# First output product's sums brought forward on VectorE, and the first norm's statistics spread over six pairs

## The chip, the cores and the metric

One core of one Trainium2 chip runs the whole kernel. The metric is the device time of one execution in microseconds. Before the change it is 1449.13 us, the median of 3 runs (1449.05 to 1449.21).

## The reference, cut to what matters

The input is x of shape (4, 1024, 512), that is 4096 tokens of width 512, and a context of 4 batches of 64 rows. Weights and results are float32.

```python
def reference(x, ctx, g_xattn, g_ffn, w_q, w_k, w_v, w_o, w_gate, w_up, w_down):
    # 16 heads of 64; keys and values come from the 64 context rows; causal mask on positions 0..63
    x = x + tanh(g_xattn) * cross_attention(layernorm(x), ctx, ctx, w_q, w_k, w_v, w_o)
    # gate, up and down projections of width 1536 with 16-bit activations and 4-bit weights
    x = x + tanh(g_ffn) * quantised_ffn(layernorm(x), w_gate, w_up, w_down)
    return x

def layernorm(x):
    return (x - mean(x)) / sqrt(var(x) + 1e-5)
```

Each of the two layer norms needs the variance of every token's row. The kernel turns the first norm's scale into a factor of the softmax's exponent (`rstd1`), so the scores are computed from raw x and the first norm is only needed when a maximum is scaled and an exponential is taken.

## The kernel before

**Stages.** A set-up stage builds the products of the context with the weights: for each batch the score matrices `m_all` and the value matrices `vwo`. The attention stage then runs over 16 *pairs* q = 0 to 15; a pair is two tiles of 128 tokens, four pairs make a batch. After it come the gate products, the up products and the down products. The change touches the end of the set-up and the attention stage.

**A pair.** Both matrix products of a pair are done in seven half-size products instead of eight, with sums around them (in the style of Strassen and Winograd). While pair q is attended, the scores of pair q+1 are made. TensorE's order is written by hand (`tc.manual_schedule`) and is, within pair q:

1. the score products 1, 6, 2, 5 of pair q+1 (L423);
2. the first turning: eight transposes of the softmax weights of pair q's first tile (L668);
3. the score products 7 and 3;
4. the second turning: the same for pair q's second tile;
5. the score product 4;
6. from q = 2 on, the transposes of two normalised tiles of an earlier group (L743);
7. the output products 1, 6, 2, 7, 5, 4, 3 of pair q (L702).

Each score product is copied (ScalarE, L429) or added (VectorE, L431) into the tile `e`. Softmax of each tile (L444 to L467) takes the masked sum where a batch begins (L444), a maximum (L449), its scaling by `rstd1` (L459), 16 exponentials, one for each head, with accumulated sums (ScalarE, L461), a reciprocal (L466), and a product with it over 128x1024 values (L467). Only then can that tile be turned. After both turnings four sums over 128x512 (L674 to L677) make the operands `eT` of the output products.

**The sums of the output products.** In `attend`, output product 1 is copied to `r` (L708). The result of each other product is added onto the token tiles `x1` and `x2` (L710), and `r` is added to the right half of `x1` after product 6 (L713) and to all of `x2` after product 2 (L716). The products 6, 7 and 4 use one PSUM bank, `oq`, one after the other: each waits until the add of the one before has read it. The add of product 7 goes onto `x2` and so comes after L716.

**Other work in the loop.** `batch_sums` (L401 to L406) makes the operand sums of a later batch, `turned_chunk` (L230 to L272) dequantises and transposes a chunk of the gate weights, `score_left` (L370 to L378) prepares the left operands of later scores, and `renormed` makes the second norm of tiles already attended (ScalarE, L730; VectorE, L738).

**Statistics and roots.** A *group* is four tiles, that is two pairs; there are eight. `stats_of(g)` loads the four tiles of group g again by SyncE's queue, one at a time into two buffers `xe` (L342), and runs a statistics and an aggregate instruction for each (L329, L332). `norm_of` turns variances into reciprocal roots: VectorE adds epsilon (L175), ScalarE takes a square root with a table load of its own (L178), and VectorE refines it (L180 to L189). In the kernel before, groups 0 and 1 have their statistics in the set-up, groups 2 and 3 ahead of the loop, groups 4 to 7 behind the pairs 0 to 3. Roots are taken for group 0 in the set-up ("a0"), for groups 1 to 3 ahead of the loop ("a1") and for groups 4 to 7 together with the second norm's root at q = 5 ("b2").

**What sets the order.** On engines other than TensorE a scheduler in the language places the instructions when the program is built, from their priorities; `tc.high_priority(SOON)` puts what it wraps ahead of other ready work, and `tc.issue_after` holds work back behind one instruction. On the chip each engine runs its list in that order.

Of the kernel before, what the change touches and what calls it, by code (L numbers as in the profile page):

```python
# [12 lines left out]
ALU = mybir.AluOpType  # L13
# [14 lines left out]
def kernel(  # L28
# [137 lines left out]
    def norm_of(pool, parts, tag):  # L166


        with tc.high_priority(SOON):
            n = sum(k.stop - k.start for _, _, _, k in parts)  # L170
            ve = pool.tile([P, n], F32, name=f"ve_{tag}", tag="ve")
            at = 0
            for rstd, off, mv, k in parts:
                w = slice(at, at + k.stop - k.start)
                nc.vector.tensor_scalar(ve[:, w], mv[:, k, 1], EPS, None, ALU.add)  # L175
                at = w.stop
            s = pool.tile([P, n], F32, name=f"s_{tag}", tag="vs")
            nc.scalar.activation(s, ve, AF.Sqrt)  # L178
            r = pool.tile([P, n], F32, name=f"r_{tag}", tag="vr")
            nc.vector.reciprocal(r, s)  # L180
            nc.vector.tensor_tensor(r, ve, r, ALU.mult)
            nc.vector.tensor_tensor(s, s, r, ALU.add)
            nc.vector.tensor_scalar(s, s, 0.5, None, ALU.mult)
            at = 0
            for rstd, off, mv, k in parts:
                w = slice(at, at + k.stop - k.start)
                nc.vector.reciprocal(rstd[:, k], s[:, w])
                if off is not None:
                    nc.vector.scalar_tensor_tensor(  # L189
                        off[:, k], mv[:, k, 0], -1.0, rstd[:, k], ALU.mult, ALU.mult  # L190
                    )
                at = w.stop
# [152 lines left out]
    def first_norm(*groups):  # L345
        return [(rstd1, None, mv1, of_group(g)) for g in groups]
# [124 lines left out]
    with tc.tile_pool(name="su", bufs=1) as su, tc.tile_pool(  # L471
# [129 lines left out]
                nc.sync.dma_start(out=xe, in_=tokens_of(g))  # L601
                group_stats(su, g, xe, True)

        norm_of(su, first_norm(0), "a0")
        for b in range(2, B):
            for k in range(2):
                nc.gpsimd.dma_start(out=m_d[b][k], in_=m_all[b][k])
# [4 lines left out]
        left[0] = score_left(0)  # L612
        for _ in batch_sums(0, 0):
            pass
        on_vector = []

        def value_matrix(b, hp, ps):

            for j in range(2):
                half = slice(j * D, (j + 1) * D)  # L620
                to = j if b % 2 == 0 else 1 - j
                nc.tensor.matmul(
                    ps[to * D : (to + 1) * D, :], vT[half, hp, b * KL : (b + 1) * KL],
                    wo[hp // 4][half, hp % 4, :], start=True, stop=True,
                )
            dst = vwo[b][hp // 4][:, hp % 4, :]
            if b != B - 1 or hp % 2 == 0:
                nc.scalar.activation(dst, ps, AF.Copy, scale=tanh_g[0])
            else:
                on_vector.append(nc.vector.tensor_scalar(dst, ps, tanh_g[0], None, ALU.mult))  # L630

        for hp in range(HP):
            for b in range(2, B):
# [6 lines left out]
    with tc.tile_pool(name="ps_s", bufs=1, space=PSUM) as ps_s, tc.tile_pool(  # L640
# [39 lines left out]
        def attend(q, a):  # L680

            b = right[1][q // QPB]
            g, i = divmod(2 * q, GRP)
            x1, x2 = xg[g][:, i, :], xg[g][:, i + 1, :]
            bank = {
                k: ps_o.tile([P, 2, HH], F32, name=f"{k}{q}", tag=k) for k in ("opn", "oq")
            }

            bank = {"op": bank["opn"][:, 0], "on": bank["opn"][:, 1], "oq": bank["oq"][:, 0]}
            r = pa.tile([P, HH], F32, name=f"r{q}", tag="r", bufs=1)  # L690

            def finished(t, x):
                nc.gpsimd.dma_start(out=x1_d[t], in_=x)
                stats(pa, x, mv2[:, t, :], f"b{t}")

            for k, at, start, dst in (
                (1, "op", True, None), (6, "oq", True, x1[:, RIGHT]), (2, "op", False, x1[:, LEFT]),
                (7, "oq", False, x2[:, RIGHT]), (5, "on", True, x2[:, RIGHT]),
                (4, "oq", False, x2[:, LEFT]), (3, "on", False, x1[:, RIGHT]),
            ):  # L700
                for h in range(HP // 2):
                    nc.tensor.matmul(  # L702
                        bank[at], a[k][:, h, :], b[k][:, h, :],
                        start=start and h == 0, stop=h == HP // 2 - 1, skip_group_check=True,
                    )
                with tc.high_priority(SOON):
                    if k == 1:
                        nc.scalar.copy(r, bank[at])  # L708
                    else:
                        ins = nc.vector.tensor_tensor(dst, bank[at], dst, add)  # L710

                if k == 6:
                    nc.vector.tensor_tensor(x1[:, RIGHT], x1[:, RIGHT], r, add)  # L713
                if k == 2:
                    v = x2.rearrange("p (n h) -> p n h", n=2)
                    nc.vector.tensor_tensor(v, v, r.unsqueeze(1).to_broadcast([P, 2, HH]), add)  # L716
                if k == 4:
                    finished(2 * q + 1, x2)
            finished(2 * q, x1)
            return ins.ins  # L720
# [38 lines left out]
        def next_left(q):  # L759
# [2 lines left out]

        ahead = scores(
            0, {6: values, 2: values, 5: lambda: values(lambda: next_left(1)), 7: values, 3: values},
            score_banks(0),
# [2 lines left out]
        next(firsts)  # L770
        next(firsts)
        softmax(0, ahead)
        with tc.issue_after(on_vector[-1].ins):
            for g in (2, 3):
                stats_of(g)
        norm_of(pa, first_norm(1, 2, 3), "a1")
        for q in range(NQ):
            b, k = divmod(q, QPB)
            turns = weights_turned(q, ahead)

            def turn():
                next(turns)
                return next(turns)


            if 0 < b < B - 1:
                if k == 0:
                    fetched(m_all[b + 1], m_d[b + 1], f"mb{b + 1}")
                if k == QPB - 1:
                    fetched(vwo[b + 1], vwo_d[b + 1], f"vb{b + 1}")  # L790
            if q == 0:
                load_group(1)
            if q % 2 == 0 and q // 2 + 2 < NG:
                load_four(xf, q // 2 + 2, xb, "x")
            if q + 1 < NQ:
                a = []
                behind = {5: turn, 3: lambda: (a.append(turn()), next_left(q + 2))}
                if q == 0:
                    behind = {**dict.fromkeys((1, 6, 2), values), 3: turn, 4: behind[3]}
                ahead = scores(q + 1, behind, score_banks(q + 1))  # L800
                if q == 0:
                    for _ in firsts:
                        pass
                softmax(q + 1, ahead)
            if q + 1 == NQ:
                turn()
                a = [turn()]
            if q > 1:
                for t in (2 * q, 2 * q + 1):
                    renormed(t - GRP)  # L810
            if q % 2 == 1 and q // 2 + 2 < NG:
                load_group(q // 2 + 2)
            if q + 1 == NQ:
                for p in range(UPB - 2):
                    ag.append(weight_sums(wgT, sg_t, p, "g"))
            added = attend(q, a[0])
            with tc.issue_after(added):
                if b + 1 < B and k in (1, QPB - 1):
                    for _ in batch_sums(b + 1, k // 2):
                        pass  # L820
            if q < NG - 4:
                stats_of(q + 4)

            if q == NQ - 2:
                norm_of(pa, [second_norm(slice(last, last + 2))], "c0")
            if q % 2 == 1 and q + 1 < NQ:
                g = q // 2
                parts = [second_norm(of_group(g))]
                if q == 5:
                    parts += first_norm(*range(4, NG))  # L830
                norm_of(pa, parts, f"b{g}")

            if 0 < q <= IC:
                oc = (q + 3) % IC
                turned_chunk(pa, oc, wgT, "g", q < 4)
                if oc > 3 and oc % 4 == 3:
                    nc.gpsimd.dma_start(out=wg_d[oc // 4 - 1], in_=wgT[oc // 4])
            if q % 4 == 0 and q < IC:
                load_four(w_gate, (q // 4 + 1) % (IC // 4), wgT, "g")
            if q == IC:  # L840
                load_four(w_up, 0, wuT, "u")
                for j in (1, 2):
                    wgT[j] = slot([P, HC, 4 * P], f"wgTb{j}")
                    nc.sync.dma_start(out=wgT[j], in_=wg_d[j - 1])
            k = q - IC
            if 0 < k < 3:
                for oc in range(2 * k - 2, 2 * k):
                    turned_chunk(pa, oc, wuT, "u")
# [705 lines left out]
```

## Time and profile before

| What | Value |
|---|---|
| median of 3 runs | 1449.13 us |
| the profiled execution's own time | 1452.2 us |
| its span | 1450.4 us |
| TensorE busy (PE) | 1406.2 us, 97% of the span |
| VectorE busy (DVE) | 1155.3 us, 80% |
| ScalarE busy (ACT) | 690.7 us, 48% |
| attention loop, from the first score product of pair 1 to that of pair 15 | 90.6 to 499.1 us |

The numbers come from one profiled execution. TensorE is the engine that is nearly always busy, so what counts is the time in which it stands idle and the time in which it is granted half its clock. In the timeline view a row gives the start, the length, the engine, the line, the instruction, what it writes and reads, the shape and the count; in brackets stands the idle time before it and what ended it. Rows on one engine overlap a little: the cost of an instruction in a row of others is the distance from its start to the next start.

### The profile page before, as it was taken

The numbers are of one execution on the slowest core, as the hardware profiler recorded it, in microseconds if no ns is written. First come the engines' busy times: TensorE is split into PE (matmuls) and PEld (weight loads), VectorE is DVE, ScalarE is ACT, GpSimd is POOL, SyncE is SP. The second block draws the span as 40 slices with busy tenths as digits, with TensorE's granted clock in tenths as the row PEclk, the third lists the DMA queues.
The fourth block names the chain that finished last, engine by engine and source line by source line (L and its number), as shares of the span: only waits on it lengthen the run. The fifth ranks groups of instructions, "written<-read, shape, count | busy, mean of one in ns | idle before, by whom it ended". The sixth has DMA issues, their size and how long they took to land. (4 is left out here: it accounts for less than half of the span.)

```text
span 1450.4 us, 15457 instructions
## 1 busy us (share of the span) xinstructions
PE 1406.2 (97%) x4884; PEld 857.6 (59%) x4884; DVE 1155.3 (80%) x2153; ACT 690.7 (48%) x1658; POOL 97.5 (7%) x191
## 2 busy tenths in 40 slices
PE   8998998999999989999999999999999999999999
PEld 6635665667667675444444444444444548888887
DVE  2777889898898899799985579888888897666632
ACT  3646576768768752000000049987886532222200
POOL 0100000000000001000000000000000110111110
PEclk9999999999999999999999999999999999999999
DMA  9675346436414215692323438958557475554321
GB/s 287 235 210 124 90 149 151 133 109 160 117 65 131 106 41 209 182 365 99 130 88 115 145 141 339 375 218 319 218 217 261 175 288 184 186 187 171 132 73 44
DMA packets 191385, 252.72 MB, mean 174 GB/s; under 512 B 125636, under 2 KB 125892, under 8 KB 185284
## 3 DMA queue, kind: packets, MB, share of 16 engines
q1 hardware_dynamic: 165828, 149.98, 33.1%
q0 software_dynamic: 18560, 76.56, 13.8%
q10 hardware_dynamic: 6912, 25.17, 4.3%
q8 instruction: 38, 0.62, 0.2%
q14 instruction: 47, 0.39, 0.1%
HBM read 142.61 MB, written 109.05 MB: 174 GB/s over the span
## 5 line engine op out<-in xcount | busy, mean ns | idle before, releaser
L461 ACT ACTIVATE e<-e,mx,rstd 128x64 f32<-128x64 f32 x416 | 177.0, 429 | 7.2 <-DVE mx L459 7.1
L886 PE MATMUL pqup<-t,wuT 128*128 128x512 f32 x192 | 91.2, 597 | 4.6 <-DVE raw_up L907 2.7
L423 PE MATMUL s<-t,xs 128*128 128x512 f32 x192 | 92.4, 604 | 0.3 <-DVE e L431 0.3
L902 ACT COPY raw_gate<-ppgate 128x512 f32<-128x512 f32 x24 | 14.1, 586 | 142.3 <-PE ppgate L886 142.3
L461 ACT ACTIVATION_READ_ACCUMULATOR e<-e,mx,rstd 128x1 f32 x416 | 78.8, 189 | 0.0
L1421 PE MATMUL ep<-wdT,upe 128*128 128x256 f32 x336 | 77.1, 379 | 0.0
L1347 ACT ACTIVATE uie<-upe,inv_up 128x1024 int16<-128x1024 f32 x48 | 53.8, 1145 | 47.7 <-DVE upe L1351 25.9
L702 PE MATMUL oq<-t,eT 128*128 128x256 f32 x256 | 64.6, 398 | 11.2 <-DVE xg L710 10.0
L1421 PE MATMUL eq<-tw,upe 128*128 128x256 f32 x312 | 72.5, 379 | 0.0
L431 DVE TENSOR_TENSOR e<-s,e 128x512 f32<-128x512 f32 x80 | 54.5, 682 | 19.3 <-PE s L423 18.9
L1421 PEld LDWEIGHTS ep<-wdT,upe 128*128 128x128 f32 x336 | 63.8, 190 | 9.1 <-DVE x1e L1400 0.2
L886 PE MATMUL ppup<-xu,wuT 128*128 128x512 f32 x144 | 67.7, 592 | 0.0
L1147 ACT ACTIVATE ar<-raw_up 128x1024 f32<-128x1024 f32 x46 | 48.3, 1052 | 40.1 <-DVE raw_up L1071 40.1
L1080 DVE TENSOR_REDUCE am_gu<-raw_up 128x1 f32<-128x512 f32 x92 | 62.4, 682 | 5.5 <-ACT raw_up L902 4.0
L886 PEld LDWEIGHTS pqup<-t,wuT 128*128 128x128 f32 x192 | 35.6, 189 | 52.3 <-issue 32.5
L894 ACT COPY raw_gate<-ppgate 128x512 f32<-128x512 f32 x24 | 14.1, 586 | 109.7 <-PE ppgate L886 75.9
L1351 DVE SCALAR_TENSOR_TENSOR upe<-uie,inv_o,gse 128x1024 f32<-128x1024 int16 (+1 forms) x50 | 60.5, 1236 | 5.1 <-ACT uie L1347 4.8
L1421 PEld LDWEIGHTS eq<-tw,upe 128*128 128x128 f32 x312 | 59.2, 190 | 8.3 <-DVE c L1439 0.3
L702 PEld LDWEIGHTS oq<-t,eT 128*128 128x128 f32 x256 | 50.3, 199 | 20.5 <-DVE xg L710 11.6
L423 PE MATMUL s<-m_all,xs 128*128 128x512 f32 x128 | 59.8, 597 | 1.5 <-DVE vwo L630 0.9
L886 PE MATMUL pqgate<-t,wgTb 128*128 128x512 f32 x128 | 60.2, 592 | 0.0
L423 PE MATMUL s<-mb,xs 128*128 128x512 f32 x128 | 59.0, 593 | 0.8 <-ACT e L429 0.8
(347 smaller groups left out, 3139.0 us busy)
## 6 DMA issues: line engine op xcount, KB each, us to landing
gate_d<-raw_gate ACTq DMA_DIRECT2D x48, 512.0 KB, 2.6
gt<-gate_d SPq DMA_DIRECT2D x48, 512.0 KB, 4.7
upe<-up_d SPq DMA_DIRECT2D x24, 1024.0 KB, 6.1
up_d<-raw_up POOLq DMA_DIRECT2D x46, 512.0 KB, 3.5
gse<-gsi_d SPq DMA_DIRECT2D x24, 512.0 KB, 4.0
gsi_d<-q SPq DMA_DIRECT2D x44, 256.0 KB, 2.7
wxT<-in_x_dram SPq DMA_DIRECT2D x128, 64.0 KB, 2.9
xg<-in_x_dram SPq DMA_DIRECT2D x8, 1024.0 KB, 6.6
```

The source lines that it names most:

```text
L423: nc.tensor.matmul(bank[at], a[k][:, h, :], b[k][:, h, :], start=start and h == 0, stop=h == HC // 2 - 1, skip_group_check=True,)
L431: nc.vector.tensor_tensor(dst, bank[at], other, add)
L461: nc.scalar.activation(ei[:, h, :], ei[:, h, :], AF.Exp, bias=mx[:, h : h + 1], scale=root, accum_out=sm[:, h : h + 1],)
L702: nc.tensor.matmul(bank[at], a[k][:, h, :], b[k][:, h, :], start=start and h == 0, stop=h == HP // 2 - 1, skip_group_check=True,)
L886: nc.tensor.matmul(bank[at], a[k][:, h, :], b[k][:, h, :], start=start and h == 0, stop=h == HC // 2 - 1, skip_group_check=True,)
L894: nc.scalar.copy(r0[:, 1, :], bank["pp"])
L902: nc.scalar.copy(r0[:, 0, :], bank["pp"])
L1080: nc.vector.tensor_reduce(am_gu[:, c, u : u + 1], r[:, c, :], AX.X, ALU.max, apply_absolute_value=True,)
L1147: nc.scalar.activation(ar, raw[u], AF.Abs)
L1347: nc.scalar.activation(ui, up[:, i, :], AF.Copy, scale=inv_u)
L1351: ins = nc.vector.scalar_tensor_tensor(o[:, i, w], ui[:, w], c_o, gs[:, i, w], ALU.mult, ALU.mult)
L1421: nc.tensor.matmul(bank[at], a[u // 2][k][:, u % 2, q % 2, :], w_of[u // 2][k][:, u % 2, :], start=start and u == 0, stop=u == UPB - 1, sk ...
```

## The change

It has two parts.

- The two adds of `r` in `attend` (L713, L716) get the high priority that the other sums have.
- The first norm's statistics and roots move. Group 1 gets its root together with group 0, in the set-up. The statistics of groups 2, 3, 4, 5, 6, 7 are placed behind pairs 0, 1, 2, 4, 6, 8. Their roots are taken in the same `norm_of` calls as the second norm's, at the first odd pair after the one behind which the statistics stand. The separate root "a1" and the hold behind the last value matrix's scaling are gone.

```diff
-        norm_of(su, first_norm(0), "a0")
+        norm_of(su, first_norm(0, 1), "a0")
...
-                on_vector.append(nc.vector.tensor_scalar(dst, ps, tanh_g[0], None, ALU.mult))
+                nc.vector.tensor_scalar(dst, ps, tanh_g[0], None, ALU.mult)
...
-                if k == 6:
-                    nc.vector.tensor_tensor(x1[:, RIGHT], x1[:, RIGHT], r, add)
-                if k == 2:
-                    v = x2.rearrange("p (n h) -> p n h", n=2)
-                    nc.vector.tensor_tensor(v, v, r.unsqueeze(1).to_broadcast([P, 2, HH]), add)
+                with tc.high_priority(SOON):
+                    if k == 6:
+                        nc.vector.tensor_tensor(x1[:, RIGHT], x1[:, RIGHT], r, add)
+                    if k == 2:
+                        v = x2.rearrange("p (n h) -> p n h", n=2)
+                        nc.vector.tensor_tensor(
+                            v, v, r.unsqueeze(1).to_broadcast([P, 2, HH]), add
+                        )
...
+        stats_behind = {2: 0, 3: 1, 4: 2, 5: 4, 6: 6, 7: 8}
...
-        with tc.issue_after(on_vector[-1].ins):
-            for g in (2, 3):
-                stats_of(g)
-        norm_of(pa, first_norm(1, 2, 3), "a1")
...
-            if q < NG - 4:
-                stats_of(q + 4)
+            for k, at in stats_behind.items():
+                if at == q:
+                    stats_of(k)
...
                 parts = [second_norm(of_group(g))]
-                if q == 5:
-                    parts += first_norm(*range(4, NG))
+                parts += first_norm(*(k for k, at in stats_behind.items() if at in (q - 1, q - 2)))
                 norm_of(pa, parts, f"b{g}")
```

More of the change, by code (lines that the diff above doesn't have):

```diff
@@ L614 @@
             pass
-        on_vector = []
         def value_matrix(b, hp, ps):
```

## The prediction

> **What bounds the kernel now.** I read the waits of TensorE first, then its timeline, then the windows of the pairs, then VectorE's timeline where TensorE waits. TensorE is busy for 97% of the span, so a gain must come out of its idle time or its clock. The waits, longest in total first:
>
> ```profile
> PE oq L702 <- DVE xg L710: 10.0, 4, 4.0
> PE ps_e L668 <- DVE e L467: 6.1, 4, 2.8
> ...
> PE ps_e L668 <- DVE mx L459: 3.3, 1, 3.3
> ```
>
> Two places in a pair: the output products that share the bank `oq`, held by VectorE's adds, and the turnings, held by the softmax. Where they lie (rows with a gap only, but for the second):
>
> ```profile
> 138.86 1.94 PE L668 MATMUL ps_e<-ident,e 128*128 128x128 f32 x8 [3.26 <-DVE mx L459]
> 140.59 3.62 PE L423 MATMUL s<-t,xs 128*128 128x512 f32 x4
> ...
> 183.59 3.78 PE L702 MATMUL oq<-t,eT 128*128 128x256 f32 x8 [3.59 <-DVE xg L710]
> ...
> 244.72 3.78 PE L702 MATMUL oq<-t,eT 128*128 128x256 f32 x8 [4.00 <-DVE xg L710]
> ...
> 302.82 1.99 PE L702 MATMUL oq<-t,eT 128*128 128x256 f32 x8 [1.19 <-DVE xg L710]
> 318.64 1.07 PE L668 MATMUL ps_e<-ident,e 128*128 128x128 f32 x8 [0.93 <-DVE e L467]
> ```
>
> After each of the three long gaps a product takes about 3.7 us instead of 1.9: half the clock. The windows of pairs 1, 2, 4 and 5, each from its first score product to the next pair's (columns: length, busy PE, PEld, DVE, ACT, POOL, then the granted clock):
>
> ```profile
> 124.26:156.56 32.30, 29.04 (x101) 19.29 (x100) 22.51 (x45) 26.93 (x118) 1.09 (x2) 0.89 0.47 114
> 156.56:189.96 33.40, 29.81 (x109) 20.34 (x108) 31.81 (x68) 19.42 (x63) 1.08 (x2) 0.90 0.43 109
> ...
> 217.02:251.24 34.22, 30.22 (x109) 20.35 (x108) 32.79 (x73) 23.52 (x85) 1.62 (x3) 0.90 0.62 140
> 251.24:277.97 26.73, 26.73 (x109) 18.44 (x108) 20.32 (x38) 21.37 (x84) 1.62 (x3) 1.00 0.43 111
> ```
>
> An undisturbed pair takes 26.73 us (25.86 before pair 2, without the 0.87 us of L743). What a pair takes above that is its excess: pair 0 2.94 (its four gaps), pair 1 6.44, pair 2 6.67, pair 3 0.32, pair 4 7.50, pair 6 1.67, pair 7 1.12, pair 10 2.72, pair 11 1.54, pair 13 0.27, in all 31.2 us. A long gap costs itself and about 3.1 us of clock (6.67 - 3.59; 6.44 - 3.26 gives 3.2). A gap of 2.80 us at 530.92 left the clock at 0.91 over 520 to 540, some 1.8 us; gaps up to 1.35 us cost nothing more.
>
> In pairs 2 and 4 VectorE is busy for 31.8 and 32.8 us, more than an undisturbed pair lasts. There the order on VectorE makes the gap. In pair 2:
>
> ```profile
> 177.34 0.41 DVE L710 TENSOR_TENSOR xg<-opn,xg 128x256 f32<-128x256 f32 x1
> ...
> 179.14 1.21 DVE L449 TENSOR_REDUCE mx<-e 128x16 f32<-128x1024 f32 x1
> 180.27 0.67 DVE L738 TENSOR_REDUCE am_x<-xm 128x1 f32<-128x512 f32 x1
> ...
> 181.59 0.41 DVE L713 TENSOR_TENSOR xg<-xg,r 128x256 f32<-128x256 f32 x1
> 181.93 0.68 DVE L716 TENSOR_TENSOR xg<-xg,r 128x512 f32<-128x512 f32 x1
> 182.53 0.70 DVE L370 STREAM_TRANSPOSE xs<-wxT 128x512 f32<-128x512 f32 x1
> 183.16 0.38 DVE L710 TENSOR_TENSOR xg<-oq,xg 128x256 f32<-128x256 f32 x1
> ```
>
> Product 7's add (183.16) comes 5.8 us after product 2's; TensorE needs it within 1.73.
>
> **Costs.** From start to next start on VectorE: L431, L329, L738, L67x 0.60; L710, L713 0.33; L449, L467, L40x 1.13; L444 1.20; L370 0.62; L466 0.16; L459 0.14; L332 0.09. One head's exponential 0.42, a copy on ScalarE 0.47 to 0.53, L730 0.76, a table load 1.28. Adding up the old order from a pair's last output add to the maximum's scaling gives 21.7, 22.8 and 20.0 us in pairs 2, 4 and 6; the trace has 21.5, 22.7 and 19.95. So the new order, which the built program shows, can be added up likewise.
>
> **The root "a1" goes.** It sat on ScalarE before pair 1's exponentials (load 108.91, reload 119.06); the first exponential came at 120.35. Without it and with eight statistics fewer ahead, the maximum of pair 1 is scaled near 109.3 instead of 118.8, and its weights are ready some 3 us before the turnings want them. Pair 1's 6.44 go. In pair 0 the sum that output product 6 needs comes about 0.45 earlier: excess 2.5.
>
> **The adds of r.** In pairs 2, 4 and 6 the new order leaves 2.2, 1.6 and 1.6 us of VectorE's work between the adds of products 2 and 7, so the waits on `oq` go: 6.67, 7.50 and most of 1.67 us. Pair 2 gets a small gap for it: the second operand sum (L675) ends at 17.4 us in the pair, product 6 could start at 16.4: 1.05.
>
> **What is late next.** The same order puts VectorE's normalisation of the second tile (L467) far back in the pairs 3, 5, 7 and 11, whose softmax begins in pairs 2, 4, 6 and 10. There the scaling of the maximum, which starts the exponentials, comes at 24.3 (before 21.7), 21.2 (23.4), 21.2 (20.2) and about 25 us (21.2), while the pair is shorter. From 24.3: load 1.28, 32 exponentials 13.4, two score copies 0.9, two weight copies 1.05, one L730 0.76 end at 41.7, 14.0 us into pair 3. The second turning wants its tile at 11.19 (six products of 1.72 and one turning of 0.87). And in all four pairs the last thing ahead of the normalisation is the add of score product 3, which itself cannot start before 11.39. Behind it, up to the end of L467 (1.22):
>
> - pair 3: L431 0.60, L738 0.59, L444 1.20, L329 0.60, L466 0.16, L332 0.09, L329 0.60, L467 1.22 = 5.06; with 0.2 from TensorE and 0.05 back, a gap of 5.3.
> - pair 5: L431, L466, L449, L467 = 3.11; gap 3.35.
> - pair 7: L431, L466, L329, L467 = 2.58, and two L370 ahead push it by 0.5: gap 3.35.
> - pair 11: L431, L375, L444, L466, L376, L467 = 3.85, VectorE 0.4 behind: gap 4.5.
>
> In the old order only one or two short steps stood there; in pair 7, the worst with 11:
>
> ```profile
> 316.24 0.68 DVE L431 TENSOR_TENSOR e<-s,e 128x512 f32<-128x512 f32 x1
> 316.84 0.24 DVE L466 RECIPROCAL rs<-sm 128x16 f32<-128x16 f32 x1
> ...
> 317.28 1.21 DVE L467 TENSOR_TENSOR e<-e,rs 128x1024 f32<-128x1024 f32 x1
> ```
>
> Those are new waits, so I bound them: if VectorE never waited and only its order counted, the gaps would be 2.3, 2.3, 2.7 and 4.1 us; as walked 5.3, 3.35, 3.35, 4.5. I take the walk, because it respects when product 3 ends. The clock after them costs between 0 and 3.4 us each; the nearest row is the same wait in pair 1, 3.26 us long, which cost 3.2, so I take 3.1. Excess: 8.4, 6.45, 6.45, 7.6.
>
> [...]
>
> **Statistics.** A group costs VectorE 2.8 us, whichever pair it stands in. Those of groups 5, 6 and 7 go to pairs 5, 7 and 9, which had room (busy 20.3, 26.9, 20.8). In pair 7 there is little, and one L329 of the four stands ahead of the late L467 (0.60, counted). Their loads wait in SyncE's queue for an `xe` buffer and hold back the gate weights, `xg`, `mb` and `vb` queued behind. The tightest is the last half of `vb` for the second batch's sums: free about 6 us into pair 7, landing in 4.9, wanted in pair 8; if that cover went, pair 8 would wait for the landing. I cost it at nothing, as I do the hold taken off the statistics. Roots: "a1" is not replaced, since "b0" to "b4" exist. In pair 10 the square root stands between the exponentials and a score copy as before, 0.4 later: excess 1.8 with a short wait at the turning.
>
> **Sum.** New excess: pair 0 2.5, 2 1.05, 3 8.4, 5 6.45, 7 6.45, 8 0.4, 9 0.1, 10 1.8, 11 7.6, 12 0.9 (L675 late, as in pair 2), 13 0.3 = 36.0 us, against 31.2: 4.8 us slower. Nothing behind the loop hides it, for TensorE runs on without a break. The profiled execution (1452.2, span 1450.4) would go to 1457.0; against the median of 1449.13 that is 1453.9.
>
> **Rivals.** *The turnings hold.* If the second tile's normalisation came in time, as a VectorE that runs well ahead would allow, the excess would be 2.5 + 1.05 + 3.5 = 7 and the time 1449.1 - 24 = 1425. For it: the old order shows short waits there. Against: the add of product 3 stands ahead of it in four pairs. Chance 0.10. *The clock stays up.* The gaps come, but half or all of them leave the clock alone: 6.2 to 12.4 us less, 1441.5 to 1447.7, so faster. It decides from two gaps on without a fall. For it: the 2.80 us gap cost only 1.8. Against: 3.26, 3.59 and 4.00 all cost 3. Chance 0.25. *ScalarE falls behind further.* A late exponential blocks VectorE's list at L466 in front of an output add, as it can in pairs 3 and 11 (L466 stands there between the adds of products 6 and 2): 1 to 3 us in each of two or three pairs, 1456 to 1461. Chance 0.15. That the change does not do what it says is out: the built order has `r`'s adds ahead of product 7's in every pair.
>
> **Numbers.** Forecast 1453.9 with chance 0.50, its own range 1450.5 to 1457.5. The 8-in-10 range is 1442 to 1459: the first rival and the ends are left out. About 0.2% (2.9 us) is what a measurement here can tell. Faster by more: the first rival and part of the second, 0.20. Within: 0.18. Slower: 0.62.
>
> **What would show it.** Right: no wait of L702 on L710 over 0.5 us; the second turnings of pairs 3, 5, 7 and 11 wait 3 to 5.5 us for L467, with the clock near 0.9 in those pairs; pairs 1, 4 and 6 last 25.9, 26.8 and 26.8. Wrong: total waits of L668 on L467 under 8 us, or these gaps at full clock, would make the change a gain; pairs 2, 4, 6 still over 28 us would make it worse.

## The result, and the profile after

The changed kernel takes 1450.62 us (median of 20 runs, 1448.67 to 1452.56) against 1448.32 us (20 runs, 1446.14 to 1450.47) for the kernel before. The ratio is 1.0016, 95% interval 1.0009 to 1.0023: slower by 2.3 us, with 1.3 to 3.3 us as the interval. That is inside the range forecast, 0.1 us above its lower end of 1450.5, and about half of the 4.8 us forecast.

The engine totals hardly move (span 1449.4 us):

```profile
PE 1403.1 (97%) x4884; PEld 856.4 (59%) x4884; DVE 1154.8 (80%) x2149; ACT 688.4 (47%) x1655; POOL 97.3 (7%) x191
```

TensorE's waits do. These are lines of the waits of the changed kernel (what waited, for whom, total us, times, longest). L666, L673, L700, L708 and L739 are the former L668, L675, L702, L710 and L738:

```profile
PE ps_e L666 <- DVE e L467: 8.5, 4, 4.4
...
PE ps_e L666 <- DVE mv L332: 8.1, 2, 5.2
...
PE ps_e L666 <- DVE mx L459: 4.2, 1, 4.2
...
PE oq L700 <- DVE eT L673: 2.6, 2, 1.3
```

The wait of the `oq` products on the adds, 10.0 us before, is not in the list. The turnings wait instead. Lines that name `mv` or `mx` mean the same wait: the profile infers who released an engine and there names a small VectorE step beside the normalisation (L467), whose end is what the turning waits for. In pair 3, for instance, the normalisation ends at 192.69 us and the turning starts at 192.83. TensorE's timeline gives the places:

```profile
165.82 1.99 PE L700 MATMUL oq<-t,eT 128*128 128x256 f32 x8 [1.34 <-DVE eT L673]
...
192.83 1.94 PE L666 MATMUL ps_e<-ident,e 128*128 128x128 f32 x8 [5.20 <-DVE mv L332]
...
252.48 1.94 PE L666 MATMUL ps_e<-ident,e 128*128 128x128 f32 x8 [4.19 <-DVE mx L459]
...
311.69 1.12 PE L666 MATMUL ps_e<-ident,e 128*128 128x128 f32 x8 [2.86 <-DVE mv L332]
...
426.79 1.94 PE L666 MATMUL ps_e<-ident,e 128*128 128x128 f32 x8 [4.43 <-DVE e L467]
```

The second to fifth rows are the second turnings of pairs 3, 5, 7 and 11. The windows of pairs 1 to 5 (length, busy PE, PEld, DVE, ACT, POOL, granted clock, DMA) show the swap: pairs 1 and 4 are undisturbed now, pairs 3 and 5 are long and at clock 0.90:

```profile
122.09:147.95 25.86, 25.86 (x101) 17.61 (x100) 19.14 (x38) 15.54 (x64) 1.09 (x2) 1.00 0.52 135
147.95:176.29 28.34, 27.00 (x110) 18.36 (x108) 27.58 (x60) 13.48 (x37) 1.08 (x2) 1.00 0.50 126
176.29:210.22 33.93, 28.73 (x110) 19.53 (x109) 27.98 (x58) 28.27 (x125) 1.62 (x3) 0.90 0.43 145
210.22:236.95 26.73, 26.73 (x110) 18.44 (x109) 26.44 (x57) 14.37 (x39) 1.08 (x2) 1.00 0.26 53
236.95:270.75 33.80, 29.61 (x109) 19.88 (x108) 25.52 (x52) 29.08 (x121) 2.17 (x4) 0.90 0.89 202
```

And VectorE's timeline in pair 3 is the list that the prediction added up, behind the add of score product 3 (187.67) to the normalisation (191.48 to 192.69):

```profile
187.67 0.69 DVE L431 TENSOR_TENSOR e<-s,e 128x512 f32<-128x512 f32 x1 [1.02 <-PE s L423]
188.29 0.69 DVE L739 TENSOR_REDUCE am_x<-xm 128x1 f32<-128x512 f32 x1
188.89 1.28 DVE L444 SCALAR_TENSOR_TENSOR e<-e,rstd,cmask 128x1024 f32<-128x1024 f32 x1
190.08 0.69 DVE L329 BATCH_NORM_STATS2 st_e<-xe 128x6 f32<-128x512 f32 x1
190.69 0.24 DVE L466 RECIPROCAL rs<-sm 128x16 f32<-128x16 f32 x1
...
190.90 0.66 DVE L329 BATCH_NORM_STATS2 st_e<-xe 128x6 f32<-128x512 f32 x1
191.48 1.21 DVE L467 TENSOR_TENSOR e<-e,rs 128x1024 f32<-128x1024 f32 x1
```

The excess of the pairs over 25.86 or 26.73 us (30.75 for pair 0) is now: pair 0 2.6, pair 2 1.6, pair 3 7.2, pair 5 7.1, pair 7 4.75, pair 10 1.9, pair 11 7.2, pair 13 0.7; in all 33.0 us, against 31.2 before.

One thing lies outside the loop: it starts at 88.77 us instead of 90.58.

### The profile page after: what moved, and what is told of

It is laid out like the page before. It is cut to its first block, busy times and chain, and to the rows that moved or that the text cites. A ratio compares the mean times of both kernels' runs of the same rounds, so it can differ in the third digit from the quotient of the medians.

```text
span 1449.4 us, 15435 instructions
## 1 busy us (share of the span) xinstructions
PE 1403.1 (97%) x4884; PEld 856.4 (59%) x4884; DVE 1154.8 (80%) x2149; ACT 688.4 (47%) x1655; POOL 97.3 (7%) x191
## 5 line engine op out<-in xcount | busy, mean ns | idle before, releaser
L423 PE MATMUL s<-t,xs 128*128 128x512 f32 x192 | 96.8, 629 | 0.2 <-DVE e L431 0.2
L431 DVE TENSOR_TENSOR e<-s,e 128x512 f32<-128x512 f32 x80 | 54.4, 680 | 21.2 <-PE s L423 20.9
L700 PE MATMUL oq<-t,eT 128*128 128x256 f32 x256 | 60.8, 380 | 2.6 <-DVE eT L673 2.6
L423 PEld LDWEIGHTS s<-t,xs 128*128 128x128 f32 x192 | 37.0, 202 | 42.6 <-issue 40.7
```

The lines of the kernel that those rows point to most:

```text
L423: nc.tensor.matmul(bank[at], a[k][:, h, :], b[k][:, h, :], start=start and h == 0, stop=h == HC // 2 - 1, skip_group_check=True,)
L431: nc.vector.tensor_tensor(dst, bank[at], other, add)
L700: nc.tensor.matmul(bank[at], a[k][:, h, :], b[k][:, h, :], start=start and h == 0, stop=h == HP // 2 - 1, skip_group_check=True,)
```

## The experiments

Theory A: the precedence of `r`'s adds trades the waits on `oq` for turn waits at a loss, and what the change gains comes from the roots. Rival B: the statistics, put behind later pairs, push the softmax back. Rival C: ScalarE's exponentials or the score product set the turnings. Each timed run stands beside runs of the kernel before on the same chip; differences in us are the ratio less 1, times the median before (1448.32 us).

**The two parts apart.** First the statistics and roots alone:

```diff
-                with tc.high_priority(SOON):
-                    if k == 6: ...  # r onto x1
-                    if k == 2: ...  # r onto x2
+                if k == 6: ...
+                if k == 2: ...
```

> The statistics and roots move as in the changed kernel; the adds of r keep their old priority. Theory A (the precedence of r's adds is what pushes the softmax back, the root 'a1' is what pair 1 gains): pair 1 loses its 6.4 us; the waits of output product 7 on oq come back in pairs 2, 4, 6 and 10 (3 to 4 us with clock in pairs 2 and 4, 2 to 2.5 us in 6 and 10), and the second turnings of pairs 3, 5, 7 and 11 wait less than 1 us; in all 3 to 7 us faster than the kernel before, about 1442 to 1446. Rival B (the statistics in pairs 1 to 9 push the softmax back): the turnings still wait 3 to 5 us in pairs 3, 5, 7, 11, the waits on oq come on top, 10 us or more slower than before.

Measured: 1443.19 us beside 1449.43, ratio 0.9961 (0.9949 to 0.9973), 5.7 us faster (3.9 to 7.4). Pair 1 lasts 25.85 us. The waits on `oq` are back, 2.87, 1.61, 2.18 and 1.37 us in pairs 2, 4, 6 and 10 and 1.0 us in 3 and 7; in pair 4 that is less than expected (PE waits):

```profile
PE oq L700 <- DVE xg L708: 10.0, 6, 2.9
PE ps_e L666 <- DVE e L467: 5.9, 4, 2.8
```

The second turnings wait 1.0 us in pairs 3 and 5, and the timeline shows no wait at those of pairs 7 and 11. A turn wait of 3.0 us in pair 10 was not expected, and its cause stays open. For the pairs 3, 5, 7 and 11 A holds and B falls.

Then the precedence alone, on the kernel before:

```diff
-                if k == 6: ...
-                if k == 2: ...
+                with tc.high_priority(SOON):
+                    if k == 6: ...
+                    if k == 2: ...
```

> Only the priority of r's adds; statistics and roots as in the kernel before. Theory A: the waits on oq in pairs 2 and 4 go (15 us with clock), pair 1 keeps its 6.4 us, and the second turnings of pairs 3, 5, 7 and 11 wait 3 to 5 us each plus 2 to 3 us of clock: 22 to 28 us; in all 6 to 12 us slower than before, about 1455 to 1461. Rival B: the waits on oq go and the turnings hold: 12 to 15 us faster than before, about 1434 to 1437.

Measured: 1458.14 us beside 1449.43, ratio 1.0061 (1.0048 to 1.0074), 8.8 us slower (7.0 to 10.7). TensorE's timeline, pairs 1, 3, 5, 7 and 11:

```profile
139.01 1.74 PE L668 MATMUL ps_e<-ident,e 128*128 128x128 f32 x8 [3.26 <-DVE mx L459]
...
200.61 1.89 PE L668 MATMUL ps_e<-ident,e 128*128 128x128 f32 x8 [4.62 <-DVE wam_g L233]
...
261.68 1.54 PE L668 MATMUL ps_e<-ident,e 128*128 128x128 f32 x8 [3.55 <-DVE e L467]
320.60 1.94 PE L668 MATMUL ps_e<-ident,e 128*128 128x128 f32 x8 [3.57 <-DVE e L467]
...
434.71 1.94 PE L668 MATMUL ps_e<-ident,e 128*128 128x128 f32 x8 [4.49 <-DVE e L467]
```

The four turn waits are there with the statistics in their old places. The pairs show the trade: pair 2 gains 6.1 us and pair 3 loses 8.1, pair 4 gains 7.5 and pair 5 loses 7.6, pair 6 gains 1.7 and pair 7 loses 4.1, pair 10 gains 1.65 and pair 11 loses 5.7. The two parts add up: 8.8 less 5.7 is 3.1, against 2.3 measured for both.

**The price of a gap.** Idle work on TensorE ahead of the late turnings:

```diff
+                fill = {3: 44, 5: 36, 7: 24, 11: 38}.get(q)
+                def second(q=q, fill=fill):
+                    if fill:
+                        keep_going(ps_s.tile([P, H], F32, name=f"idle{q}", tag="s0"), fill)
+                    a.append(turn())
+                    next_left(q + 2)
-                behind = {5: turn, 3: lambda: (a.append(turn()), next_left(q + 2))}
+                behind = {5: turn, 3: second}
```

> The changed kernel with idle transposes (44, 36, 24, 38 of them, results unused) on TensorE ahead of the second turning of the pairs 3, 5, 7 and 11, to fill the gaps without shortening them. If the price of a gap is its own length and a stretch at half clock after it: the clock stays at 1.00 in these pairs, each is 2.0, 2.9, 1.9, 2.8 us shorter, 9.6 us in all, about 1441. If what the pairs lose beyond the gap is late work and not the clock: no change, 1450.6. If the filling overshoots the moment when the tile is ready: up to 1 us longer in a pair, 1452.

Measured: 1443.30 us beside 1449.43, ratio 0.9960 (0.9947 to 0.9973), 5.8 us faster than before and so about 8 us faster than the changed kernel (9.6 expected). Pair 3 in TensorE's timeline and in the windows:

```profile
187.19 4.97 PE L295 MATMUL idle<-ident 128*128 128x128 f32 x44
192.15 1.07 PE L666 MATMUL ps_e<-ident,e 128*128 128x128 f32 x8
```

```profile
176.00:208.15 32.15, 32.00 (x154) 23.09 (x152) 27.47 (x57) 24.93 (x109) 1.10 (x3) 1.00 0.53 164
```

The turning starts 16.2 us into the pair (16.5 without the transposes), so the gap is filled and not shortened by much; but it takes 1.07 us instead of 1.94, the clock stays at 1.00, and the pair is 1.8 us shorter. The four pairs together lose 18.6 us instead of 26.2. Of these 7.7 us, 6.7 lie behind the start of the turning, where the clock acts, and 1.0 ahead of it. (The scheduler planned VectorE's list anew, so not every pair is step for step that of the changed kernel.) The clock is a real term of the price; without it the change would be faster than the kernel before as it stands, as the prediction said. The kernel before loses to the clock too, 8.9 us in its trace (see the table below), and its gaps were not filled, so this is no comparison of equals.

**The softmax first.** Would precedence for the maximum cure it?

```diff
-            nc.vector.tensor_reduce(mx, ei, AX.X, ALU.max)
+            with tc.high_priority(SOON):
+                nc.vector.tensor_reduce(mx, ei, AX.X, ALU.max)
...
-                nc.vector.tensor_scalar(mx, mx, root, -1.0, ALU.mult, ALU.mult)
+                with tc.high_priority(SOON):
+                    nc.vector.tensor_scalar(mx, mx, root, -1.0, ALU.mult, ALU.mult)
```

> The changed kernel, with the softmax maximum (L449) and its scaling (L459) given precedence on VectorE, which brings the scaling from 21 to 25 us in the pair to 13 to 15 us. Theory A (VectorE's order between a pair's output adds and the scaling sets the turn gaps): the second turnings of pairs 3, 5, 7 and 11 wait less than 1 us, which takes 26 us out; but the operand sums (L675) of pairs 2, 4, 6, 10, 11 end later, and output product 6 waits about 4.5, 2.2, 2.4, 0.6, 2.3 us there, 12 to 15 us with clock: 11 to 14 us faster than the changed kernel, about 1437 to 1440. Rival C (the exponentials on ScalarE or the add of score product 3 set the turnings): they wait as before, and the new waits come on top, 1462 or more.

Measured: 1450.37 us beside 1449.43, ratio 1.0010 (1.0001 to 1.0020). A miss: it was expected to be 11 to 14 us faster than the changed kernel, and within the noise it is no faster. The turn waits of the pairs 1 to 13 did go, so C falls as well: VectorE's order sets the turnings. But the operand sums behind them are late instead, more than I had added up (PE waits):

```profile
PE oq L702 <- DVE eT L675: 20.3, 8, 4.5
```

Output product 6 waits 4.45, 3.00, 3.21, 2.58, 2.61 and 2.48 us in pairs 2, 3, 4, 6, 10 and 11, 18.3 us in all where I had expected 12.0. I had expected 0.6 in pair 10 and none in pair 3.

**Load moved.** About 4.7 us of VectorE work per batch, issued one pair earlier, on the changed kernel:

```diff
-                if b + 1 < B and k in (1, QPB - 1):
-                    for _ in batch_sums(b + 1, k // 2):
-                        pass
+                for kk in (1, QPB - 1):
+                    if b + 1 < B and k == (kk - 1 if kk in (1,) else kk):
+                        for _ in batch_sums(b + 1, kk // 2):
+                            pass
```

> The changed kernel with the operand sums of the next batch's score matrices (L401 to L406, about 4.7 us of VectorE) issued one pair earlier, behind the last output add of pairs 0, 4, 8 instead of 1, 5, 9; they ran in pairs 2, 6 and 10. If VectorE's load in a pair sets how late the scaling of the maximum comes: the turn waits in pairs 3, 7 and 11 fall from 5.2, 2.9, 4.4 us to under 0.5 us (19 us with clock), and new ones come in the pairs behind those that got the load, 2, 5 and 10, of about 3.4, 4.5 and 3.2 us with 2 to 3 us of clock each (about 18 us, against the 7 us that pair 5 loses now); in all 6 to 9 us faster than the changed kernel, about 1442 to 1445. If the load does not matter: the waits stay in pairs 3, 5, 7, 11 and the time at 1451.

Measured: 1444.45 us beside 1448.38, ratio 0.9978 (0.9967 to 0.9989), 3.2 us faster than before, about 5.5 faster than the changed kernel (6 to 9 expected). The turn waits of pairs 3, 7 and 11 went; new ones of 3.47 and 3.55 us came in pairs 2 and 10 (3.4 and 3.2 expected), pair 5 kept one of 3.39 (4.5 expected, 4.19 in the changed kernel), and one of 2.61 us for an operand sum came in pair 3, not expected. The load moved and the waits moved with it.

**The roots alone**, on the kernel before:

```diff
-        norm_of(su, first_norm(0), "a0")
+        norm_of(su, first_norm(0, 1), "a0")
...
-        norm_of(pa, first_norm(1, 2, 3), "a1")
...
+                if q == 1:
+                    parts += first_norm(2, 3)
```

> The kernel before, without the separate root ahead of the loop: group 1's root goes with group 0's, those of groups 2 and 3 with the second norm's at q = 1. Statistics and the adds of r stay. If the root alone holds up pair 1's exponentials: pair 1 lasts 25.9 instead of 32.3 us, the waits on oq in pairs 2 and 4 stay at 3.5 to 4 us with their clock, 5 to 7 us faster than before, about 1443. If the eight statistics of groups 2 and 3 ahead of the loop are what makes pair 1 late: pair 1 keeps a turn wait of 2 us or more, and the kernel is at most 2 us faster than before.

Measured: 1440.51 us beside 1448.38, ratio 0.9951 (0.9937 to 0.9964); and once more:

> The kernel with only the roots moved, once more, beside the run before: the same 7 to 8 us faster than the kernel before, 1440 to 1441.

1440.89 us beside 1448.87, ratio 0.9944 (0.9930 to 0.9957). This beats both kernels, by 7 to 8 us the one before and by 9 to 10 the changed one. Pair 1 lasts 25.85 us, though the eight statistics still stand ahead of the loop; the first maximum is scaled at 114.62 us there, which is early enough.

Which half of the root's move does it? The root ahead of the loop kept, for groups 2 and 3:

```diff
-        norm_of(su, first_norm(0), "a0")
+        norm_of(su, first_norm(0, 1), "a0")
...
-        norm_of(pa, first_norm(1, 2, 3), "a1")
+        norm_of(pa, first_norm(2, 3), "a1")
```

> The kernel before, with group 1's root taken with group 0's in the set-up; the separate root ahead of the loop stays, for groups 2 and 3 alone. All five kernels so far that take group 1's root in the set-up start the loop at 88.4 to 88.9 us, the two that don't at 90.6 and 90.7. If that root is the cause: the loop starts near 88.7, and with pair 1's wait unchanged (3.26 us and clock) the kernel is 1.9 us faster than before. If the root ahead of the loop is held up by group 1's part of it: pair 1's wait goes too, up to 8 us faster. If the earlier start comes from what else those kernels change: the loop starts at 90.6 and the time is that of before.

Measured: 1443.79 us beside 1448.87, ratio 0.9962 (0.9948 to 0.9976), 5.5 us faster. The loop starts at 88.57 us and pair 1 lasts 25.86. The root is still there, 2.0 us earlier than in the kernel before, and the reload for the exponentials comes 2.4 us earlier (116.64, before 119.06), in ScalarE's timeline:

```profile
106.89 1.28 ACT L178 ACT_TABLE_LOAD   x1
108.19 0.21 ACT L178 ACTIVATE s_a<-ve_a 128x8 f32<-128x8 f32 x1
...
116.64 1.28 ACT L461 ACT_TABLE_LOAD   x1 [5.71 <-DVE mx L459]
```

Pair 0 lasts 36.07 us instead of 33.82 with the roots alone (33.69 before): an operand sum is 1.97 us late and the clock falls (the output product behind it takes 3.47 us; with the roots alone 1.99, behind 1.48 us). So moving group 1's root into the set-up brings most of the gain, with the separate root and its table load still ahead of the loop: some 2.0 us by the earlier start, and 6.4 us in pair 1 against 2.4 us lost in pair 0. Dropping the rest of "a1" brings some 2 us more, though the intervals overlap.

**Trying for more.** The statistics alone with idle transposes in the two longest gaps:

```diff
+                if (q, k) == (2, 7): keep_going(..., 24)   # ahead of the output product
...
+                fill = {10: 25}.get(q)                     # ahead of the second turning
```

> The statistics and roots alone (no precedence for r's adds), with idle transposes on TensorE in the two longest gaps: 24 of them ahead of output product 7 in pair 2, 25 ahead of the second turning in pair 10. These gaps were 2.87 and 3.00 us and were followed by 3.4 and 6.8 us at half clock. If the clock is what the pairs lose beyond the gaps: 1.7 and 3.4 us less, about 1438. If not: 1443.

Measured: 1445.69 us beside 1448.38, ratio 0.9981 (0.9972 to 0.9990): 2.8 us faster than before, not the 11 expected, and less than without the transposes. The clock fell in neither of the two pairs (in pair 2 output product 7 takes 1.99 us, without the transposes 2.53), which took 2.5 and 2.9 us less. But the scheduler gave VectorE another order, and new waits of 2.32 and 2.17 us came in pairs 3 and 4. As a test of the clock it is spoilt. And the roots alone with some statistics in later pairs:

```diff
+        stats_behind = {4: 0, 5: 1, 6: 7, 7: 8}    # two groups later
+        stats_behind = {5: 4, 6: 7, 7: 8}          # three; group 4 ahead of the loop
```

> The kernel with only the root moved, and in addition the statistics of groups 6 and 7 behind the pairs 7 and 8 instead of 2 and 3, their roots at q = 9; groups 4 and 5 stay behind pairs 0 and 1. If VectorE's load in the crowded pairs 3 and 4 makes the wait on oq in pair 4: it falls from 2.8 to about 1.4 us and the short wait in pair 3 goes, a wait on oq of about 1.9 us comes in pair 8, pair 2 keeps its 3.4 us; 2 to 4 us faster than with the root alone, about 1437 to 1439. If the load only moves the waits along: pairs 8 to 10 lose what 3 and 4 gain, 1440 to 1442.

> As the run with two groups moved, but group 4's statistics ahead of the loop and group 5's behind pair 4, so that pairs 1 to 4 hold none. By VectorE's order: wait on oq in pair 2 about 1.4 us (3.4 with the root alone), in pair 4 about 1.4 us, in pair 6 about 3.8 us (1.6), in pair 8 about 1.9 us, second turning of pair 10 about 1.7 us; 1438 to 1441 if the waits in pairs 6 to 10 cost clock, 1436 if not.

Measured: 1443.16 and 1443.22 us beside 1448.05, ratios 0.9965 (0.9952 to 0.9979) and 0.9967 (0.9955 to 0.9978): both faster than before, neither better than the roots alone. Pairs 3 and 4 of the first gained 2.0 and 4.7 us against the roots alone; pairs 8, 9 and 10 lost 1.2, 1.2 and 3.8. In the second, pairs 2, 3 and 4 gained 2.6, 1.4 and 4.9 us; pairs 0, 6 and 10 lost 1.8, 3.3 and 5.2, of which only a part was forecast. Again the load moved the waits along.

**Where the loop's time is.** The loop runs from the first score product of pair 1 to that of pair 15. For each trace I summed TensorE's gaps in it, and half of TensorE's busy time within the stretches that the trace records at half clock (the two kernels with idle transposes are left out, for these count as busy):

| Kernel | Loop us | Gaps | Lost to clock | Rest |
|---|---|---|---|---|
| before | 408.6 | 19.3 | 8.9 | 380.4 |
| changed | 410.4 | 22.4 | 8.9 | 379.1 |
| statistics and roots | 405.0 | 19.9 | 4.7 | 380.4 |
| precedence alone | 416.0 | 27.4 | 9.1 | 379.6 |
| maximum first | 410.4 | 23.3 | 7.2 | 379.9 |
| sums one pair early | 405.0 | 18.6 | 6.5 | 379.9 |
| roots alone, first run | 400.5 | 18.0 | 1.6 | 381.0 |
| roots alone, second run | 401.6 | 16.4 | 4.5 | 380.7 |
| two groups later | 401.4 | 17.3 | 3.3 | 380.9 |
| three groups later | 404.4 | 17.7 | 5.1 | 381.6 |
| group 1's root alone | 403.3 | 17.2 | 5.9 | 380.2 |

The rest is the same within 2.5 us. In the loop the difference between the kernels is gaps and clock, and nothing else of size. What follows the loop lasts 947.9 to 952.0 us in the 13 traces.

## Why the prediction was right, and where it was off

- **Direction and mechanism: right.** The waits on `oq` went, the second turnings of the four named pairs came in their place, and pairs 1, 4 and 6 last 25.85, 26.73 and 26.73 us. The scaling of the maximum in pairs 2, 4, 6 and 10 starts 24.5, 21.1, 20.9 and 24.7 us into the pair (24.3, 21.2, 21.2 and about 25 forecast). The clock is 0.90 in pairs 3, 5 and 11; in pair 7, whose wait is just under the 3 us named, it is 0.95. The run with the precedence alone shows that the precedence, not the statistics, makes the turn waits.
- **The gaps: right in sum; two were off, and their errors partly cancel.** Forecast 5.3, 3.35, 3.35 and 4.5 us, measured 5.20, 4.19, 2.86 and 4.43: 16.5 against 16.7 in all. The walk through VectorE's built order, with the durations of the old trace, carried it; the bounds by order alone (2.3, 2.3, 2.7, 4.1) were too low in each. Pair 5 has the steps forecast, but the add of score product 3 starts at 249.27 us, 12.3 us into the pair instead of 11.4: just ahead of it VectorE waits twice for 0.56 us, up to 245.27 and 246.53, for loads of `xe`, which the prediction cost at nothing. In pair 7 the two L370 push that add by 0.2 us and not 0.5.
- **Pair 1: right in its time, incomplete in its reason.** The maximum is scaled at 107.45 us; named were 109.3, and the set-up below explains the 1.8 us between. The prediction named the separate root and eight fewer statistics. The statistics were not needed, for both runs of the roots alone have the gain with all eight in place; nor was the whole separate root, for pair 1's wait goes even with groups 2 and 3 still in it.
- **The clock: the term that was mis-sized.** I took 3.1 us for each of the four gaps, 12.4 in all. The pairs lost 2.0, 2.9, 1.9 and 2.8 us beyond their gaps, 9.6 in all. That is 2.8 of the 3.0 us by which the excess of 36.0 was too high (33.0 measured). The row that the price was taken from does not keep it either: in the run with the precedence alone, pair 1 has the same wait of 3.26 us and loses 1.9 us beyond it, not 3.2. The rival in which the clock stays up had part of the truth: the price of a gap is not fixed. The section on the hardware shows one gap at two prices.
- **The set-up: a term that was missing.** The loop starts 1.8 us earlier, which the sum did not have. Before, VectorE waits 1.83 us, up to 45.70 us, for the square root of "a0", and L561 stands behind it in VectorE's list; TensorE waits 1.59 us at 47.51 us for L561 and then has a stretch at half clock (49.36 to 52.78 us). With group 1's root in "a0" the table load moves from 44.16 to 53.32 us (in the trace of the roots alone). That wait and the half clock are gone, and a later wait for L561, of 1.19 us at 55.64, shows. The run with the precedence alone, which keeps the old root, has both waits and no half clock there (the 16 matmuls of L530 at that place take 3.72 us, before 4.61). All the kernels run here with group 1's root in the set-up start the loop at 88.1 to 89.2 us, the two without at 90.6 and 90.7.
- **One execution against the median.** The profiled execution before took 1452.2 us, 3.9 over the median of the 20 runs and more than any of them; that after took 1451.2, 0.6 over its own. So the two traces differ by 1.0 us in favour of the change, and the medians by 2.3 against it. A difference of this size cannot be read from one trace on each side. Here lies the luck in the forecast: the clock and the set-up together take 4.6 us off the 4.8 forecast, and in the traces the loop does end at the same time (499.13 and 499.17 us). That the medians still differ the way that was forecast goes back to the 3.3 us by which the execution before lay further above its median than the one after, and that the prediction did not know. The mechanism does not hang on this, for the parts taken alone differ by 8.8 and 5.7 us.
- **ScalarE falling behind** added nothing that the four gaps do not hold: they sum to what was forecast without it. Nor did the hold and the loads queued behind `xe` cost anything in pairs 8 and 9, which are undisturbed.

What the change could have been: its roots bring 7 to 8 us, its precedence costs 8.8, and spreading the statistics brings nothing that the runs show (5.7 us faster with the roots, against 7.1 and 8.1 for the roots alone; the intervals overlap).

## What to carry to other kernels

VectorE is busy for 25.8 us of each pair on average (pairs 0 to 13) in the run with statistics and roots alone, and an undisturbed pair lasts 26.73. On an engine as full as that, precedence did not cure the waits here, twice over (for `r`'s adds and for the maximum): putting one step first made another late. So ask for every step brought forward which consumer now stands last, and add up the built order to its end. What helped was moving work out of the way: group 1's root into the set-up, and the rest of the separate root into the later `norm_of`s, which exist anyway.

## What the runs showed of the hardware

**One gap had two prices.** In the traces of the two kernels the stretches at half clock last 3.41 us (four of them) or 6.83 us (six), but for one that the end of each span cuts off. The same kernel (the roots alone) ran twice, with the same gap of 3.40 us in pair 2. In the first run the clock stayed at 1.00, and output product 7 behind the gap takes 1.99 us; a shorter gap of 2.80 us, in pair 4, was followed by 3.41 us at half clock, and the product behind it takes 3.52 us (windows of 3.41 us; the clock is the third number from the end):

```profile
170.75:174.16 3.41, 1.61 (x8) 1.08 (x6) 3.41 (x8) 3.40 (x12) 0.00 (x0) 1.00 0.74 277
174.16:177.57 3.41, 1.81 (x8) 1.63 (x9) 3.38 (x9) 3.41 (x17) 0.00 (x0) 1.00 0.01 2
232.18:235.60 3.42, 0.92 (x5) 0.46 (x3) 3.42 (x8) 3.41 (x14) 0.00 (x0) 1.00 0.81 126
235.60:239.01 3.41, 3.12 (x7) 2.50 (x8) 2.38 (x10) 3.41 (x17) 0.00 (x0) 0.50 0.85 216
```

In the second run the gap of pair 2 was followed by two such windows at half clock, and the product behind it takes 3.78 us; the pair took 33.97 us instead of 30.91:

```profile
172.24:175.65 3.41, 0.62 (x3) 0.19 (x1) 3.41 (x7) 3.40 (x17) 0.00 (x0) 1.00 0.75 239
175.65:179.06 3.41, 2.80 (x7) 2.27 (x8) 2.90 (x8) 3.41 (x18) 0.00 (x0) 0.50 0.05 20
179.06:182.48 3.42, 3.42 (x10) 2.70 (x9) 2.69 (x5) 3.42 (x19) 0.54 (x1) 0.50 0.02 8
```

So the same gap cost 0 us of clock in one execution and 3.1 us in another. Nor did the longer gap cost more: with the maximum first, output product 6 takes 2.00 us behind a gap of 3.21 us in pair 4 and 3.54 us behind one of 3.00 us in pair 3, and with group 1's root alone 3.47 us behind one of 1.97 us in pair 0. In these runs the length of a gap alone does not give its price.

**What stays open.** Whether the average price of the old and new gaps, taken over many executions, gives the 2.3 us exactly was not tried. Nor do the runs show why one gap costs clock and another does not, or why what follows the loop differs by up to 4 us from trace to trace, more than the change is worth.
